# Scores by query in a transformer block: sixteen products of 32 by 32 in place of four of 32 by 128

## The chip, the cores and the metric

The kernel runs on one core of one Trainium2 chip. The metric is the device time of one execution in microseconds; shorter is better.

## The reference

A transformer block with adaptive layer norm (a condition gives shift, scale and gate for each of the two halves) on x of 8 x 1024 x 512, float32 throughout, 16 heads of 32 channels, causal attention, and a feed-forward part of 2048 channels:

```python
mod = silu(condition) @ Wada + bada
sh_a, sc_a, gt_a, sh_m, sc_m, gt_m = split(mod, 6, axis=1)
xn = layernorm(x, g1, be1)
xm = xn * (1 + sc_a) + sh_a
# attention, heads of 32 channels
scores = einsum('bhqd,bhkd->bhqk', q, k) * hd ** -0.5
attn = softmax(where(causal, scores, -inf))
out = einsum('bhqk,bhkd->bhqd', attn, v)
x = x + gt_a * (out @ Wproj + bproj)
xn = layernorm(x, g2, be2)
xm = xn * (1 + sc_m) + sh_m
h = gelu(xm @ W1 + b1)
x = x + gt_m * (h @ W2 + b2)
```

## The kernel before

The 8 sequences of 1024 tokens are cut into 16 blocks of 512 tokens (`n`; `h` says whether it is the first or the second block of its sequence). A block's queries and keys lie transposed in `qTs[n]` and `kTs[n]`: 128 partitions by 4 groups `g` by 512 tokens. A group is four heads, `HPG = 4`, of `hd = 32` channels, so head `j` of a group lies on the partitions 32j to 32j+31. In `qTs[n][r, gg, ...]` the slice `r` picks the head, `gg` the group, and the last index the tokens; `P` is 128, `TB` 512, and `SQ` (set for another purpose) 32.

Each softmax is made in two rounds. The first, scores by query, only finds the maximum of each row: `score_units` lists the work, `scores_at_once` (the edited function) makes scores with queries on the partitions and keys along the free dimension in `sc`, a tile of 128 x 4 x 512 that fills four PSUM banks, one for each head; VectorE adds the causal mask on the diagonal (L1745) and takes the maximum over the keys (L1748). The maxima are turned into rows (L1786). The second round, `weights_T`, makes the scores again with keys on the partitions (L1812 puts minus the maximum in, L1824 adds the scores) in `st`, ScalarE takes the exponential (L1837), GpSimd masks the diagonal and sums (L1842, L1950), and `weigh` multiplies by the values (L1865). `sc` and `st` share one buffer (the tag "st" has one).

One call of `scores_at_once` handles 512 columns of `sc` for a tile of 128 queries: one part of 512 columns, or on the diagonal 512, 384 + 128, or 256 + 256 columns (two groups). For each part it issues four products, one a head, whose stationary operand is 32 channels by 128 queries and whose moving operand is 32 channels by `w` keys. They occupy four separate row groups of TensorE's array. All linear layers (`matmul`, L233) instead use four products of 128 channels by 32 columns, in four column groups of the array; so do L1786, L1865 and L1886 (the sums of the weights). L1812 and L1824 use rows, like the scores.

The order of the work is written out by the kernel's own planner at build time: it keeps estimated times for each engine (`note_pe`, `note`), mixes the linear layers as a background stream with attention (`step_aside`, `work`, `pace`), and puts each step into the one queue of its engine. A stretch of scores therefore stands between stretches of linear layers.

Of the kernel before, what the change touches and what calls it, by code (L numbers as in the profile page):

```python
# [22 lines left out]
def kernel(  # L23
# [33 lines left out]
    nc = tc.nc  # L57
    B, T, D = x.shape
    HD = W1.shape[1]
    P = 128  # L60
    hd = D // H
# [6 lines left out]
    HPG = P // hd  # L68
# [62 lines left out]
    def note(engine, ns, reads=(), writes=(), port=False):  # L131
        start = max(now[engine], due(reads, writes))
        if port:
            start = max([start] + [b for a, b, *_ in pool_spans if a <= start < b])
            give_way(start, start + ns - FREE)
        elif engine == "POOL":
            start = max([start] + [b for a, b in port_spans if a <= start < b])
        end = start + ns
        now[engine] = end
        if port:  # L140
            port_spans.append((start, end - FREE))
            del port_spans[:-16]
        elif engine == "POOL":
            pool_spans.append((start, end, reads, writes))
            del pool_spans[:-16]
        for k in reads:
            left[k] = max(left.get(k, 0.0), end + SYNC)
        for k in writes:
            written[k] = end + SYNC
        return end  # L150

    def note_pe(ns, form, reads=(), writes=()):
        now["PE"] = max(now["PE"], due(reads, writes))
        if shape[0] != form:
            shape[0] = form
            now["PE"] += SWITCH
        note("PE", ns, reads)
        spent[0] += ns
        for k in writes:
            written[k] = now["PE"] + PIPE  # L160
# [80 lines left out]
    SQ = 32  # L241
# [43 lines left out]
    for w in range(1, NB):  # L285
        n = w - 1
# [26 lines left out]
    n = NB - 1  # L313
# [577 lines left out]
    qTs, kTs, vs = {}, {}, {}  # L891
# [699 lines left out]
    def step_aside(reads, writes):  # L1591


        while threads():
            if linear_wait() == NEVER:
                hurry()
            own, other = wait_of((reads, writes)), linear_wait()
            if done_linear[0] < stream["due"]:
                if other > own + 100:
                    break  # L1600
            elif own <= max(other, 50):
                break
            work()
        while BANK in writes and bank_at() == NEVER:
            work()
        run_jobs()
        run_pool_jobs()
        run_transfers()
        run_preparation()
# [52 lines left out]
    def keys_of(n, kh):  # L1662
        return kTs[n - blocks[n][1] + kh]

    def diagonals(parts, sc):

        if parts[-1][4] == parts[0][4]:
            first, span = parts[0][3] - P, len(parts) * P
            return span, sc[:, :, first : first + span]
        return 2 * P, sc.rearrange("p j (a c) -> p j a c", c=2 * P)[:, :, :, P:]  # L1670

    def scores(n, g, parts):

        h = blocks[n][1]
        for gg in {part[4]: None for part in parts}:
            if (n, gg) not in maxima:
                maxima[n, gg] = small.tile([P, 2, NTT, HPG], F32, tag="mx", name=f"mx_{n}_{gg}")
        reads = [("qT", n), ("kT", n - h + parts[0][1])]
        if (
            linear_wait() > 3000  # L1680
            and not any(live)
            and wait_of((reads, ["st"])) > wait_of((reads, [BANK])) + 1000
        ):
            scores_by_heads(n, g, parts, reads)
        else:
            scores_at_once(n, g, parts, reads)
        if units[unit_at[0] + 1 :] == [] or units[unit_at[0] + 1][:2] != (n, g):
            split_maxima(n, g, h)
# [35 lines left out]
    def scores_at_once(n, g, parts, reads):  # L1724
        h = blocks[n][1]
        step_aside(reads, ["st"])
        sc = ps_st.tile([P, HPG, TB], F32, tag="st", name=f"sc_{n}_{g}_{parts[0][0]}_{parts[0][1]}")
        for qt, kh, c0, w, gg in parts:
            for j in range(HPG):
                r = slice(j * hd, (j + 1) * hd)  # L1730
                nc.tensor.matmul(  # L1731
                    sc[:, j, c0 : c0 + w],
                    qTs[n][r, gg, ts(qt, P)],
                    keys_of(n, kh)[r, gg, :w],
                    start=True,
                    stop=True,
                    skip_group_check=True,
                )
            note_pe(2 * COLUMN * w, "rows", reads, ["st"])
        if parts[0][1] == h:  # L1740
            span, place = diagonals(parts, sc)
            shape_of = mask[:, :span].unsqueeze(1)
            if len(place.shape) == 4:
                shape_of = shape_of.rearrange("p o (a c) -> p o a c", c=P)
            nc.vector.tensor_tensor(place, place, shape_of.to_broadcast(place.shape), ALU.add)  # L1745
            note("DVE", 165 + 4.16 * span, ["st"])
        for qt, kh, c0, w, gg in parts:
            nc.vector.tensor_reduce(  # L1748
                maxima[n, gg][:, kh, qt, :], sc[:, :, c0 : c0 + w], axis=AX.X, op=ALU.max
            )  # L1750
            note("DVE", 170 + 4.14 * w, ["st"], [("mx", n, gg)])
# [383 lines left out]
```

## Time and profile before

| what | value |
|---|---|
| time, median of 3 runs | 3463.61 us (3462.65 to 3463.67) |
| the profiled execution | 3465.39 us, span of its trace 3463.7 us |
| granted TensorE clock | 0.999 |
| TensorE (PE) busy | 3424.3 us, 99% of the span |
| its weight loads (PEld) busy | 1776.1 us |
| VectorE (DVE), ScalarE (ACT), GpSimd (POOL) busy | 2069.1, 1288.6, 1940.4 us |
| passes of the edited line on TensorE | 329.2 us busy, 3072 records |

An instruction group is written as line, engine, operation, output and inputs by the program's tile names, output and input size (partitions x elements), number of instructions, then busy time in us, mean duration in ns, and the idle time ahead of it with what ended it. For TensorE a form such as `32*128` is the rows and columns of the array that an instruction uses, followed by the moving operand. PE are the passes of the moving operand, PEld the loads of the stationary one. In the timeline the first number is the start and the second the duration, from the first start to the last end of the merged instructions; passes overlap one another, since their ends include the way through the array.

### The profile page before, as it was taken

How to read it: one execution, taken by the hardware profiler on the slowest of the kernel's cores; microseconds unless marked ns; L12 is line 12 of the kernel's file. 1: busy time of each engine (PE TensorE's matmuls, PEld its weight loads, DVE VectorE, ACT ScalarE, POOL GpSimd, SP SyncE). 2: the span in 40 equal slices, each digit the busy share in tenths (PEclk: the TensorE clock that was granted, in tenths of full speed). 3: DMA queues.
4: the chain of work that ended last, by engine and by line, in shares of the span. 5: the costliest groups of instructions: out<-in, count | busy, mean ns of one | idle time of the engine just before them, and what ended most of it. 6: DMA issues, size and time to landing. Idle time of an engine off the chain costs nothing.

```text
span 3463.7 us, 122539 instructions
## 1 busy us (share of the span) xinstructions
PE 3424.3 (99%) x55442; PEld 1776.1 (51%) x55442; DVE 2069.1 (60%) x2295; ACT 1288.6 (37%) x1422; POOL 1940.4 (56%) x2090
## 2 busy tenths in 40 slices
PE   8999999999999999999999999999999999999999
PEld 5544554455544554455554455454554545544555
DVE  6765666646566465664657546575566745556364
ACT  2345234343243433434333352433524334242421
POOL 3666757756267572774626755277553774446530
PEclk9999999999999999999999999999999999999999
DMA  6843444345644455444544445444464454633444
GB/s 220 273 135 87 121 113 130 105 123 148 175 135 129 128 150 161 133 141 128 163 145 136 136 134 169 138 133 139 132 182 130 125 147 124 190 110 87 120 144 137
DMA packets 379613, 489.93 MB, mean 141 GB/s; under 512 B 28388, under 2 KB 235548, under 8 KB 379092
## 3 DMA queue, kind: packets, MB, share of 16 engines
q1 hardware_dynamic: 378896, 481.80, 47.1%
q8 instruction: 437, 7.16, 0.9%
q14 instruction: 84, 0.69, 0.1%
q10 hardware_dynamic: 196, 0.28, 0.0%
HBM read 428.44 MB, written 53.53 MB: 139 GB/s over the span
## 4 chain that ended last, share of the span: by engine, by line
PE 90%; DVE 4%; ACT 2%; DMA 2%; issue 1%; POOL 1%; SPq 0%; DVEq 0%; ACTq 0%; POOLq 0%
PE bank L233 62%; PE sc L1731 8%; PE po L1865 7%; PE st L1824 7%; PE st L1812 3%; DVE mx L1748 2%; PE bank L1886 2%; ACT pT L1837 1%; DMA w<-kept_up_S 1%; DVE sc L1745 1%; DMA xm_m<-turned_m 1%; PE bank L1786 1%; DVE hT L1321 0%; ACT hT L1252 0%; PE bank L847 0%
## 5 line engine op out<-in xcount | busy, mean ns | idle before, releaser
L1950 POOL TENSOR_TENSOR pT<-pT,pT 128x256 f32<-128x256 f32 (+3 forms) x1254 | 1221.5, 1009 | 148.5 <-ACT pT L1837 119.4
L1837 ACT ACTIVATE pT<-st 128x2048 f32<-128x2048 f32 x288 | 541.1, 1879 | 1006.9 <-PE st L1824 905.9
L233 PE MATMUL bank<-w,hT 128*32 128x256 f32 x14336 | 813.9, 380 | 0.0
L1748 DVE TENSOR_REDUCE mx<-sc 128x4 f32<-128x2048 f32 (+3 forms) x384 | 665.7, 1754 | 201.1 <-PE sc L1731 194.9
L233 PEld LDWEIGHTS bank<-w,hT 128*32 128x32 f32 x14336 | 454.4, 110 | 357.9 <-issue 75.7
L233 PE MATMUL bank<-xm_m,w 128*32 128x256 f32 x8192 | 499.5, 380 | 1.2 <-issue 0.7
L1842 POOL TENSOR_SCALAR_AFFINE_SELECT pT<-pT 128x512 f32<-128x512 f32 x256 | 180.5, 723 | 368.2 <-ACT pT L1837 366.4
L233 PE MATMUL bank<-t_m,w 128*32 128x256 f32 x6144 | 383.9, 381 | 1.0 <-DVE mx L1748 0.5
L233 PEld LDWEIGHTS bank<-xm_m,w 128*32 128x32 f32 x8192 | 256.4, 110 | 226.0 <-issue 60.9
L1731 PE MATMUL sc<-kT,qT 32*128 32x512 f32 (+3 forms) x3072 | 329.2, 520 | 3.5 <-DVE mx L1748 3.0
L1745 DVE TENSOR_TENSOR sc<-sc,mask 128x1024 f32<-128x1024 f32 (+1 forms) x160 | 162.8, 1017 | 250.7 <-PE sc L1731 179.4
L1865 PE MATMUL po<-pT,v 128*32 128x512 f32 (+3 forms) x3072 | 304.8, 491 | 0.5 <-POOL pT L1842 0.5
L1824 PE MATMUL st<-qT,kT 32*128 32x512 f32 (+3 forms) x3072 | 300.1, 486 | 0.0
L233 PEld LDWEIGHTS bank<-t_m,w 128*32 128x32 f32 x6144 | 190.0, 110 | 179.4 <-issue 53.1
L233 PE MATMUL bank<-xm_a,w 128*32 128x256 f32 x3968 | 241.0, 381 | 2.0 <-ACT xm_a L862 1.1
L190 POOL TENSOR_TENSOR qT<-top,rec 128x512 f32<-128x512 f32 x60 | 78.3, 1304 | 282.7 <-ACT rec L1904 279.0
L222 DVE TENSOR_TENSOR hT<-bank,u_u 128x512 f32<-128x512 f32 x192 | 130.2, 687 | 153.6 <-PE bank L233 151.0
L1731 PEld LDWEIGHTS sc<-kT,qT 32*128 32x128 f32 x3072 | 129.5, 183 | 162.1 <-issue 56.8
L233 PE MATMUL bank<-w,qT 128*32 128x256 f32 (+1 forms) x2944 | 192.4, 399 | 0.7 <-DVE p_proj L214 0.7
L233 PE MATMUL bank<-t_a,w 128*32 128x256 f32 x2944 | 179.4, 380 | 0.4 <-DVE qT L222 0.4
L233 PEld LDWEIGHTS bank<-xm_a,w 128*32 128x32 f32 x3968 | 127.7, 110 | 99.1 <-issue 17.9
L1252 ACT ACTIVATE hT<-hT,cols 128x512 f32<-128x512 f32 x256 | 164.1, 711 | 23.1 <-DVE hT L222 22.4
(238 smaller groups left out, 3408.4 us busy)
## 6 DMA issues: line engine op xcount, KB each, us to landing
w<-in_L_cond_W_dram SPq DMA_DIRECT2D x384, 256.0 KB
w<-kept_up_S SPq DMA_DIRECT2D x256, 256.0 KB
w<-kept_down_S SPq DMA_DIRECT2D x256, 256.0 KB
w<-kept_qkv_S SPq DMA_DIRECT2D x180, 256.0 KB
w<-in_L_cond_Wqkv_dram SPq DMA_DIRECT2D x147, 256.0 KB
hat<-in_x_dram SPq DMA_DIRECT2D x64, 256.0 KB
xr<-in_x_dram SPq DMA_DIRECT2D x64, 256.0 KB
out_dram<-xr SPq DMA_DIRECT2D x64, 256.0 KB
```

The source lines that it names most:

```text
L222: nc.vector.tensor_tensor(out, src, other, op)
L233: nc.tensor.matmul(ps[r], columns, rhs, start=start, stop=stop, skip_group_check=True)
L1252: nc.scalar.activation(hT[:, i, :], hT[:, i, :], AF.Gelu, bias=cols[:, O_B1 + f : O_B1 + f + 1])
L1731: nc.tensor.matmul(sc[:, j, c0 : c0 + w], qTs[n][r, gg, ts(qt, P)], keys_of(n, kh)[r, gg, :w], start=True, stop=True, skip_group_check=True,)
L1745: nc.vector.tensor_tensor(place, place, shape_of.to_broadcast(place.shape), ALU.add)
L1748: nc.vector.tensor_reduce(maxima[n, gg][:, kh, qt, :], sc[:, :, c0 : c0 + w], axis=AX.X, op=ALU.max)
L1812: nc.tensor.matmul(st[:, j, c0 : c0 + w], minus_ones[r, :], row[r, TB - w :], start=(c0 == 0), stop=False, skip_group_check=True,)
L1824: nc.tensor.matmul(st[:, j, c0 : c0 + w], kT[r, gg, ts(k % NTT, P)], qT[r, gg, TB - w :], start=False, stop=True, skip_group_check=True,)
L1837: nc.scalar.activation(pT[:, :, :used], st[:, :, :used], AF.Exp, scale=scale)
L1842: nc.gpsimd.affine_select(diagonal, diagonal, pattern=[[0, HPG], [1, P]], compare_op=ALU.is_ge, fill=0.0, base=0, channel_multiplier=-1,)
L1865: nc.tensor.matmul(po[r, TB - w :], v[:, k % NTT, g * P + j * hd : g * P + (j + 1) * hd], pT[:, j, c0 : c0 + w], start=(k == 0), stop=last ...
L1950: nc.gpsimd.tensor_tensor(into, into, pT[:, j, c0 : c0 + w], ALU.add)
```

## The change

Each of the four products of a part (32 channels by 128 queries) is split into four along the queries: sixteen products of 32 channels by 32 queries, each writing 32 partitions of one bank of `sc`. The outer loop goes over the four sets of 32 queries, the inner one over the four heads as before. What the planner is told (`note_pe`) is the same.

```diff
         for qt, kh, c0, w, gg in parts:
-            for j in range(HPG):
-                r = slice(j * hd, (j + 1) * hd)
-                nc.tensor.matmul(
-                    sc[:, j, c0 : c0 + w],
-                    qTs[n][r, gg, ts(qt, P)],
-                    keys_of(n, kh)[r, gg, :w],
-                    start=True,
-                    stop=True,
-                    skip_group_check=True,
-                )
+            for a in range(P // SQ):
+                for j in range(HPG):
+                    r = slice(j * hd, (j + 1) * hd)
+                    nc.tensor.matmul(
+                        sc[ts(a, SQ), j, c0 : c0 + w],
+                        qTs[n][r, gg, ts(qt * (P // SQ) + a, SQ)],
+                        keys_of(n, kh)[r, gg, :w],
+                        start=True,
+                        stop=True,
+                        skip_group_check=True,
+                    )
             note_pe(2 * COLUMN * w, "rows", reads, ["st"])
```

## The prediction

> **What bounds the kernel now.** I read the page first: the busy shares, the chain that ended last, and the costliest groups.
>
> ```profile
> span 3463.7 us, 122539 instructions
> PE 3424.3 (99%) x55442; PEld 1776.1 (51%) x55442; DVE 2069.1 (60%) x2295; ACT 1288.6 (37%) x1422; POOL 1940.4 (56%) x2090
> PE 90%; DVE 4%; ACT 2%; DMA 2%; issue 1%; POOL 1%; SPq 0%; DVEq 0%; ACTq 0%; POOLq 0%
> PE bank L233 62%; PE sc L1731 8%; PE po L1865 7%; PE st L1824 7%; PE st L1812 3%; DVE mx L1748 2%; PE bank L1886 2%; ACT pT L1837 1%; DMA w<-kept_up_S 1%; DVE sc L1745 1%; DMA xm_m<-turned_m 1%; PE bank L1786 1%; DVE hT L1321 0%; ACT hT L1252 0%; PE bank L847 0%
> L1837 ACT ACTIVATE pT<-st 128x2048 f32<-128x2048 f32 x288 | 541.1, 1879 | 1006.9 <-PE st L1824 905.9
> L1748 DVE TENSOR_REDUCE mx<-sc 128x4 f32<-128x2048 f32 (+3 forms) x384 | 665.7, 1754 | 201.1 <-PE sc L1731 194.9
> ```
>
> TensorE is busy 99% of the span and is 90% of the chain, so what the edited line L1731 takes on TensorE is paid almost one to one; it is 8% of the chain, some 280 us. The engines that consume the scores sit idle waiting for TensorE (the L1748 row: 194.9 of 201.1 us), so they set nothing here. How many stretches of scores there are I take from the instructions grouped with shapes kept apart:
>
> ```profile
> L1731 PE MATMUL sc<-kT,qT 32*128 32x512 f32 x1536 | 219.0, 640 | 2.7 <-DVE mx L1748 2.3
> L1731 PE MATMUL sc<-kT,qT 32*128 32x384 f32 x512 | 59.4, 533 | 0.0
> L1731 PE MATMUL sc<-kT,qT 32*128 32x256 f32 x512 | 36.7, 400 | 0.7 <-DVE mx L1748 0.7
> L1731 PE MATMUL sc<-kT,qT 32*128 32x128 f32 x512 | 25.6, 269 | 0.0
> L1731 PEld LDWEIGHTS sc<-kT,qT 32*128 32x128 f32 x3072 | 129.5, 183 | 162.1 <-issue 56.8 <-ACT pT L1837 45.0 <-DVE mx L1748 20.7
> ```
>
> Each program product is two records here, a first and a second pass over the moving operand (float32), each with its own weight load; a part of four products is 8 records. That makes 192 stretches of 512 columns alone, 64 of 384 + 128 and 32 of 256 + 256 (64 parts): 288 stretches of 512 columns each, one per call of scores_at_once, as many as the 288 exponentials of the transposed scores.
>
> **What one stretch costs.** The timeline of TensorE around one of the 192, then narrower windows on it, on its loads, and on a long stretch of L233.
>
> ```profile
> 1000.65 1.48 PE L233 MATMUL bank<-w,t 128*32 128x256 f32 x24
> 1002.06 1.14 PE L1731 MATMUL sc<-kT,qT 32*128 32x512 f32 x8
> 1003.13 0.64 PE L233 MATMUL bank<-w,t 128*32 128x256 f32 x8
> 1003.58 0.39 PE L233 MATMUL bank<-w,qT 128*32 128x256 f32 x3
> ...
> 1002.06 0.18 PEld L1731 LDWEIGHTS sc<-kT,qT 32*128 32x128 f32 x1 [0.41 <-ACT pT L1837]
> 1002.06 0.20 PEld L1731 LDWEIGHTS sc<-kT,qT 32*128 32x128 f32 x4 [0.41 <-ACT pT L1837]
> 1002.59 0.61 PE L1731 MATMUL sc<-kT,qT 32*128 32x512 f32 x4
> ...
> 1007.50 2.77 PE L233 MATMUL bank<-w,qT 128*32 128x256 f32 x48
> 1010.09 0.61 PE L1886 MATMUL bank<-pT,ones 128*32 128x512 f32 x4
> ```
>
> The 48 passes of L233 run from 1007.50 to 1010.09: six sets of eight (four side by side, twice) in 2.59 us, so 0.216 us for a pass of 256 columns and 0.43 for one of 512. The stretch of scores lasts from 1002.06 to 1003.13, 1.07 us: its first passes take 0.53 (1002.06 to 1002.59) and its second passes 0.54 until the next form may start. Over 2 x 0.43 that is 0.10 us of load in front (128 columns of queries, before anything streams) and 0.11 of emptying the array at the change of form, in which the last product's lag is contained. That lag: one load lasts 0.18, the four together 0.20, so three steps are 0.02 us, some 6.7 ns per product (5 to 8.3 by the rounding). The load of a form of 32 columns shows at 1003.13: its two passes of 256 columns last until 1003.58, 0.45 against 0.43 without a change of form, so 0.02 us.
>
> **The change, part by part.**
>
> Streaming. Four products of 32 by 128 fill the array; sixteen of 32 by 32 fill it too. All four row groups side by side are shown by L1731 itself, all four column groups by L233, and both at full rate. If all sixteen run side by side a pass stays 0.43 us: no change.
>
> The exposed load. It shrinks from 128 columns to 32: by the L233 entry it is 0.02 us in place of 0.10, minus 0.08 us per stretch, 23 us over 288.
>
> The stagger. Sixteen products start one behind the other where four did: fifteen steps in place of three, 12 x 6.7 ns = plus 0.08 us per stretch (0.06 to 0.10), 23 us over 288. It lies on the path, because the last product must finish before the form can change, and every stretch of scores has another form on both sides (L233 in the timeline). The step covers four instructions (load, pass, load, pass); I take it for products 5 to 16 as for 1 to 4, since nothing wider is in the trace, and keep both bounds.
>
> Within the 96 stretches of two parts the second part's loads and starts lie under the first part's passes (256 columns take 0.216 us, sixteen steps 0.11), so nothing is added.
>
> Instructions. L1731's 3072 passes and 3072 loads become 12288 of each, 18432 more instructions.
>
> ```profile
> q8 instruction: 437, 7.16, 0.9%
> L233 PEld LDWEIGHTS bank<-w,hT 128*32 128x32 f32 x14336 | 454.4, 110 | 357.9 <-issue 75.7
> 224.81 0.41 PE L1786 MATMUL bank<-ident_b,mcols 128*32 128x128 bf16 x16
> 225.03 0.61 PE L1865 MATMUL po<-pT,v 128*32 128x512 f32 x4
> ```
>
> 7.16 MB for 110884 loads and passes is 65 bytes each, so 1.2 MB more on a queue with a share of 0.9%: covered by the slack of the DMA engines. Later loads of 110 ns each lie beside passes as in L233. What is not covered is a slow feed of the 64 instructions at the head of a stretch. The fastest stretch that is dense throughout is L1786: 16 passes and 16 loads from 224.81 to 225.03, 6.9 ns per instruction, but there the passes themselves may be what sets it; the first four products of a stretch of scores take 1.7 ns per instruction (6.7 / 4). I take 1.7, which the nearer row shows, and keep 6.9 for a rival.
>
> The rest. The change moves no step, adds no DMA and no wait: the scores' tile, its readers, and the costs told to the planner are the same, so the written order on all engines stays. The maximum (L1748) and the mask (L1745) start after the last product as before.
>
> The sum: -0.08 + 0.08 = 0.00 us per stretch, between -0.02 and +0.02; over 288, between -6 and +6 us. The profiled execution took 3465.39 us with a span of 3463.7, 1.8 us over the median of 3463.61; I carry the difference to the median and forecast 3463 us. Something like 0.2%, 7 us, is what a measurement of this kernel tells from no change; that is 24 ns per stretch, or a step of 8.7 ns in place of 6.7.
>
> **The rivals.**
>
> Slower: the feed. TensorE's instructions arrive more slowly than 1.7 ns once the 16 at the head are used up. Product 16 has 60 instructions ahead of it; at 1.7 ns they take 0.10 us. From 2.1 ns on the loss is over 24 ns per stretch and the kernel is slower. At 3 ns product 16 starts at 0.18, +0.08 us, +23 us in all (3487); at the 6.9 ns of L1786 it starts at 0.41, +0.31, +90 us (3554). For it: four times the instructions come in the time that sixteen took, and no row shows 64 that fast. Against it: TensorE has 1.07 us of earlier work in which to run ahead. The Trainium skill (TensorE: Matmul & The Clock Gate, Part 1, on the 56 ns gap) has a floor that speaks against this change: starts of passes never come closer than about 25 ns. This trace does not agree, with four loads 0.02 us apart in all; by the page, 32 starts would last 0.8 us and a stretch about 1.3.
>
> Slower by much: waiting second passes hold up the products behind them. In the compiled program a product's second pass follows its first directly; that the four first passes nevertheless start within 0.02 us, and the second ones 0.53 later, shows that products on other tiles overtake up to three waiting passes. Whether they overtake fifteen, no row shows. If only four may wait, each set of four starts when the set before begins its second passes: five passes in place of two, +3 x 0.43 = 1.29 us, +370 us (3835). The Trainium skill (same page, Part 3, The mechanism) says that matmuls keep program order in start and end. The four here would then take five passes, 2.15 us, and they take 1.07, so the trace does not agree; for sixteen it would be seventeen passes.
>
> Faster: the step is shorter. The bfloat16 ones of L1812 start closer together:
>
> ```profile
> 1005.85 0.10 PEld L1812 LDWEIGHTS <-minus_ones 32*128 32x128 bf16 x4 [0.41 <-issue]
> L1812 PEld LDWEIGHTS <-minus_ones 32*128 32x128 bf16 x1536 | 31.5, 91 | 138.9 <-issue 89.3 <-DVE mx L1748 36.8 <-DVE mx L1762 2.5
> ```
>
> Four loads of 91 ns in 0.10 us are steps of 3 ns, for two instructions a product. If the step hangs on the product and not on its number of instructions, fifteen steps are 0.05 us, -0.05 net, -14 us (3449); if the lag costs nothing, because it lies under the emptying of 0.11, the whole load is won, -23 us (3440). The Trainium skill (same page, Part 3, measured speedup) gives about 4 ns per tile and a speedup of 10.6 for sixteen tiles; by it the gain would be about 12 us. No run here shows sixteen.
>
> That the change would not do what it says I see no room for: the slices are the same elements of queries, keys and scores.
>
> **How the numbers follow.** The forecast, balance within 6 us: 0.45. The feed: 0.25, most of it at the small end. Second passes that hold up: 0.10. The shorter step: 0.20. So faster 0.20, same 0.45, slower 0.35. The range from 3446 to 3492 holds the forecast, the faster case to beyond 3 ns a step, and the feed up to 3.3 ns per instruction; it leaves out the 0.10 of held-up passes, the costlier end of the feed (about 0.05) and the full gain of the load (about 0.05).
>
> **What would show it.** In the profile after, L1731 has 12288 passes and loads, of forms 32*32. Around one stretch the timeline should show the sixteen loads starting within 0.10 us, the second passes starting about 0.45 after the first, and the next form 1.07 after the beginning. Starts spread over more than 0.13 us show the feed; second passes of the first products before the first passes of the last show the hold-up, with a stretch of 2 us or more; a stretch under 1.04 shows the shorter step. The span's difference should be 288 times the stretch's difference; anything else, above all new waits on TensorE, would make this account wrong even where the time fits.

## The result

The changed kernel takes 3499.97 us (median of 4 runs, 3498.93 to 3502.4) against 3463.64 us before: slower by 36.3 us, a ratio of 1.0106 with a 95% interval of 1.0094 to 1.0119. The forecast was 3463, and the range ended at 3492.

The page of the changed kernel, the lines that answer to those shown of before (the edited line is now L1732):

```profile
span 3498.5 us, 140971 instructions
PE 3460.1 (99%) x64658; PEld 1774.9 (51%) x64658; DVE 2062.6 (59%) x2295; ACT 1288.8 (37%) x1422; POOL 1943.4 (56%) x2090
PE bank L233 64%; PE sc L1732 9%; PE po L1866 7%; PE st L1825 7%; PE st L1813 3%; PE bank L1887 2%; DVE mx L1749 2%; ACT pT L1838 1%; DMA w<-kept_up_S 1%; DMA xm_m<-turned_m 1%; PE bank L1787 0%; DVE sc L1746 0%; PE bank L847 0%; ACT hT L1252 0%; PE bank L582 0%
q8 instruction: 509, 8.34, 1.0%
L1732 PE MATMUL sc<-kT,qT 32*32 32x512 f32 (+3 forms) x12288 | 366.6, 492 | 3.1 <-DVE mx L1749 3.0
```

TensorE is still what bounds the kernel, with 36 us more of it busy; the other engines do what they did. The edited line alone is busy for 37 us more (366.6 after, 329.2 before). The passes by shape, shapes kept apart:

```profile
L1732 PE MATMUL sc<-kT,qT 32*32 32x512 f32 x6144 | 223.1, 599 | 2.8 <-DVE mx L1749 2.7
L1732 PE MATMUL sc<-kT,qT 32*32 32x384 f32 x2048 | 61.8, 493 | 0.0
L1732 PE MATMUL sc<-kT,qT 32*32 32x128 f32 x2048 | 52.8, 278 | 0.0
L1732 PE MATMUL sc<-kT,qT 32*32 32x256 f32 x2048 | 47.8, 385 | 0.3 <-DVE mx L1749 0.3
```

The calls of one part (512 columns) gained 4 us busy (219.0 before). The three shapes that occur only in calls of two parts gained 41 when their rows are added; 384 and 128 columns overlap in time, so this is more than the line gained as a whole. Among them the 128 columns, which come second, doubled (25.6 before). So the timeline is to be read in two places. First a call of one part: the whole of it, then cut off behind its first pass, behind the fourteenth, behind the sixteenth, and behind the seventeenth, which is the first of the second passes:

```profile
589.95 1.16 PE L1732 MATMUL sc<-kT,qT 32*32 32x512 f32 x32
591.04 0.85 PE L233 MATMUL bank<-w,qT 128*32 128x256 f32 x12
...
589.95 0.61 PE L1732 MATMUL sc<-kT,qT 32*32 32x512 f32 x1
589.95 0.70 PE L1732 MATMUL sc<-kT,qT 32*32 32x512 f32 x14
589.95 0.73 PE L1732 MATMUL sc<-kT,qT 32*32 32x512 f32 x16
589.95 1.04 PE L1732 MATMUL sc<-kT,qT 32*32 32x512 f32 x17
```

It lasts 1.09 us where it was 1.07 (1.087 and 1.071 in the trace's nanoseconds). All sixteen products run side by side. The first fourteen start within 0.09 us (0.70 less 0.61 for one pass), thirteen steps of 6.7 ns, and the last two need 0.03 for two more. The row with x17 is that of a view that closes at 590.41: the second passes begin 0.45 us into the call, 0.43 of streaming and 0.02 of load. Now a call of 384 + 128 columns, its passes, its loads, and its loads from the 35th on; below it one of before:

```profile
620.39 1.50 PE L1732 MATMUL sc<-kT,qT 32*32 32x384 f32 x64
621.81 0.42 PE L233 MATMUL bank<-w,hT 128*32 128x256 f32 x4
...
620.39 0.46 PEld L1732 LDWEIGHTS sc<-kT,qT 32*32 32x32 f32 x33 [0.41 <-ACT pT L1838]
621.06 0.55 PEld L1732 LDWEIGHTS sc<-kT,qT 32*32 32x32 f32 x31 [0.22 <-issue]
621.25 0.36 PEld L1732 LDWEIGHTS sc<-kT,qT 32*32 32x32 f32 x30
```

```profile
613.24 1.15 PE L1731 MATMUL sc<-kT,qT 32*128 32x384 f32 x16
614.32 0.42 PE L233 MATMUL bank<-w,hT 128*32 128x256 f32 x4
613.24 0.96 PEld L1731 LDWEIGHTS sc<-kT,qT 32*128 32x128 f32 x16 [0.41 <-ACT pT L1837]
```

This call takes 1.42 us where it took 1.08. Of its 64 loads, the 32 of the first part and one of the second come early, one more at 621.06, and the other thirty only from 621.25 on, 0.86 us into the call. Even the last tile had finished streaming the first part by then: twice 384 columns are 0.64 us, and the starts are spread over 0.12. And once they come they come slowly: thirty loads in 0.36 - 0.10 = 0.26 us, 17 ns for the four instructions of a product, 4.3 ns each, where the head of the call had 1.7. The view names no other engine that the loads waited for: it has "issue" (nothing that the profile shows) ahead of the one at 621.06, and nothing ahead of the thirty.

192 calls with 0.016 us more and 96 with 0.34 more are 3 + 33 = 36 us, which is the measured difference. Every one of the 96 shows the same wait.

### The profile page after: what moved, and what is told of

It reads as the page before. It is cut to its first block, busy times and chain, and to the rows that moved or that the text cites. A ratio compares the mean times of both kernels' runs of the same rounds, so it can differ in the third digit from the quotient of the medians.

```text
span 3498.5 us, 140971 instructions
## 1 busy us (share of the span) xinstructions
PE 3460.1 (99%) x64658; PEld 1774.9 (51%) x64658; DVE 2062.6 (59%) x2295; ACT 1288.8 (37%) x1422; POOL 1943.4 (56%) x2090
## 4 chain that ended last, share of the span: by engine, by line
PE 93%; DVE 3%; ACT 2%; DMA 1%; issue 1%; POOL 0%; SPq 0%; DVEq 0%; ACTq 0%; POOLq 0%
PE bank L233 64%; PE sc L1732 9%; PE po L1866 7%; PE st L1825 7%; PE st L1813 3%; PE bank L1887 2%; DVE mx L1749 2%; ACT pT L1838 1%; DMA w<-kept_up_S 1%; DMA xm_m<-turned_m 1%; PE bank L1787 0%; DVE sc L1746 0%; PE bank L847 0%; ACT hT L1252 0%; PE bank L582 0%
## 5 line engine op out<-in xcount | busy, mean ns | idle before, releaser
L1732 PE MATMUL sc<-kT,qT 32*32 32x512 f32 (+3 forms) x12288 | 366.6, 492 | 3.1 <-DVE mx L1749 3.0
L1732 PEld LDWEIGHTS sc<-kT,qT 32*32 32x32 f32 x12288 | 129.2, 103 | 176.6 <-issue 70.3
```

The costliest lines, as they stand in the source:

```text
L1732: nc.tensor.matmul(sc[ts(a, SQ), j, c0 : c0 + w], qTs[n][r, gg, ts(qt * (P // SQ) + a, SQ)], keys_of(n, kh)[r, gg, :w], start=True, stop=True,
```

## The experiments

Theory "window": TensorE takes in instructions in program order and holds about 64 of them, counted from the oldest one that is not finished. A part with sixteen products is 64 instructions (load, pass, load, pass for each). By the theory the second part of a call stays outside until products of the first are finished, and then comes in at the rate at which instructions are fed, 4.3 ns each. The call of 384 + 128 columns above shows where that comes from: the first product's second pass starts at 0.34 us (0.02 of load and 0.32 of streaming), and by the rows by shape a pass of 384 columns lasts 0.49 us with its way through the array, so this product is finished at 0.83; the held loads start at 0.86. (The ends of passes are modelled by the profiler, the starts are recorded.) Two rivals: "feed", a loss in proportion to the added instructions, and "same tiles", a second part that cannot follow the first closely on the same tiles of the array.

**e1_one_part and e2_two_part: the change in one kind of call alone.** The number of queries to a product is chosen by the kind of call:

```diff
-            for a in range(P // SQ):
+            SW = SQ if len(parts) == 1 else P      # e2: P if len(parts) == 1 else SQ
+            for a in range(P // SW):
...
-                        sc[ts(a, SQ), j, c0 : c0 + w],
-                        qTs[n][r, gg, ts(qt * (P // SQ) + a, SQ)],
+                        sc[ts(a, SW), j, c0 : c0 + w],
+                        qTs[n][r, gg, ts(qt * (P // SW) + a, SW)],
```

Expected of e1_one_part:

> Sixteen products only in the 192 calls of one part; four products, as before, in the 96 calls of two parts. Theory 'window': TensorE looks no further than about 64 instructions behind its oldest unfinished one, and a call of one part with sixteen products is just 64 instructions; it loses only the 16 ns that the trace after shows (1.087 us in place of 1.071), so +3 to +5 us, about 3467 us. Rival 'feed' (the loss goes with the number of added instructions, of which half are in these calls): half of the 36 us, about 3482 us. Rival 'same tiles' (a second part cannot follow the first closely on the same tiles of the array, whatever the number of instructions): as the window, 3467 us.

Expected of e2_two_part:

> Sixteen products only in the 96 calls of two parts, four in the others. Window: 128 instructions in a call, twice what TensorE looks over; the call takes 1.42 us in place of 1.08, so +33 us, about 3497 us. Feed: half of the 36 us, about 3482 us. Same tiles: 3497 us.

Measured: e1_one_part 3471.02 us, ratio 1.0019 (1.0010 to 1.0028); e2_two_part 3494.48 us, ratio 1.0088 (1.0074 to 1.0101). The two halves have the same number of added instructions and lose 7.4 and 30.8 us, so the loss does not go by instructions: feed alone is out. The losses add up, 38 for 36. The one-part kernel lost 7.4 us (3.5 to 9.7 by the interval) where 3 to 5 were expected; its trace shows 4.0 us more span than before (3467.7 us) and the same 1.087 us calls, so some 3 us of its median no view accounts for. "Same tiles" expects the same as the window of these two kernels; the next two tell them apart.

**e3_eight: eight products of 32 by 64 in every call.** Half the products, so that both parts of a call are 64 instructions:

```diff
-            for a in range(P // SQ):
+            SW = 2 * SQ
+            for a in range(P // SW):
```

> Eight products of 32 channels by 64 queries in every call. A part is 32 instructions, a call of two parts 64. Window: nothing waits beyond the window; the load in front is that of 64 columns (0.05 us, half of 0.10), the stagger seven steps of 6.7 ns (0.05) in place of three (0.02), so a call takes 1.04 us in place of 1.07 to 1.08, -0.03 x 288 = -8 us, about 3455 us: faster than before. Feed: a third of the added instructions of the sixteen (6144 of 18432), +12 us, less the 8: about 3468 us. Same tiles: the second part of the 96 calls waits as it does with sixteen, at least the 0.18 us by which its second product comes late there, +17 us, less the 8: about 3473 us.

Measured: 3456.41 us, ratio 0.9979 (0.9970 to 0.9988): 7.2 us faster than before, 43.6 faster than the change. Its timeline, a call of one part, one of 384 + 128 and that one's loads:

```profile
578.07 1.11 PE L1733 MATMUL sc<-kT,qT 32*64 32x512 f32 x16
579.11 0.42 PE L233 MATMUL bank<-w,qT 128*32 128x256 f32 x4
...
608.33 1.12 PE L1733 MATMUL sc<-kT,qT 32*64 32x384 f32 x32
609.38 0.42 PE L233 MATMUL bank<-w,hT 128*32 128x256 f32 x4
608.33 0.88 PEld L1733 LDWEIGHTS sc<-kT,qT 32*64 32x64 f32 x32 [0.41 <-ACT pT L1839]
```

1.04 and 1.05 us: the second part follows the first without a pause on the same tiles, so "same tiles" is out for tiles of 32 by 64. Both rivals had this kernel slower than before; only the window had it faster. The gain of 0.03 us per call fits the load of 64 columns in place of 128, less the stagger of eight products in place of four, as the expectation sums them.

**e4_sets_outside: the same instructions in another order.** In calls of two parts each set of 32 queries has both its parts before the next set begins:

```diff
         for qt, kh, c0, w, gg in parts:
-            for a in range(P // SQ):
+            note_pe(2 * COLUMN * w, "rows", reads, ["st"])
+        for a in range(P // SQ):
+            for qt, kh, c0, w, gg in parts:
                 for j in range(HPG):
...
-            note_pe(2 * COLUMN * w, "rows", reads, ["st"])
```

The planner is told the same for each part, now ahead of the products.

> Sixteen products, but in the calls of two parts the loop over the four sets of 32 queries stands outside the loop over the parts; the same instructions in another order. Window: the first 64 instructions now hold both parts of two sets, so the other two sets start only when products of the first sets are finished, at about 0.85 and 1.1 us; a call of two parts takes about 2.1 us in place of 1.42, +0.7 x 96 = +69 us over the changed kernel, about 3569 us. Feed: the same number of instructions, 3500 us. Same tiles: the sets that have not started wait for no tile, so at most as long as now, 3500 us or less.

Measured: 3566.7 us (one run). A call of 384 + 128 columns:

```profile
634.97 2.22 PE L1734 MATMUL sc<-kT,qT 32*32 32x384 f32 x64
637.12 0.42 PE L233 MATMUL bank<-w,hT 128*32 128x256 f32 x4
...
634.97 0.85 PEld L1734 LDWEIGHTS sc<-kT,qT 32*32 32x32 f32 x34 [0.41 <-ACT pT L1839]
635.83 1.10 PEld L1734 LDWEIGHTS sc<-kT,qT 32*32 32x32 f32 x30
...
635.12 0.10 PEld L1734 LDWEIGHTS sc<-kT,qT 32*32 32x32 f32 x1
635.50 0.10 PEld L1734 LDWEIGHTS sc<-kT,qT 32*32 32x32 f32 x1
```

It takes 2.15 us. Half of the array has nothing to do, the loads for it are next in the program, and yet thirty of them start only from 0.86 us on, as in the changed kernel, behind the 64 instructions of the first two sets. What holds them is their place in the program, not their tile.

The last two rows are the two loads of the third set's first product, the seventeenth, alone in narrow windows. Its first load is over at 0.26 us and its tile is idle, but its first pass, instruction 66, starts only at 0.53, with the second load right behind it. Instruction 2, 64 places before that pass, is the first pass of the call, which ends at about 0.50 (0.49 us by its row by shape); instruction 4, the second pass of the same product, ends at 0.83, and the loads from instruction 69 on start at 0.86. In all 64 calls of this shape both steps lie 0.03 us behind the end of that earlier pass. So places are given back one after the other in program order, and 64 is their number as these calls show it; 32 passes would be the same count, since here every pass has a load of its own.

**e5_halves16 and e6_halves4: calls of one part as two halves of 256 keys.** Is it the number of instructions, or the diagonal and the second group that are special to calls of two parts?

```diff
+            SW = SQ                                # e6: SW = P
+            pieces = [(0, w)] if len(parts) > 1 else [(0, w // 2), (w // 2, w // 2)]
+            for k0, kw in pieces:
-            for a in range(P // SQ):
+                for a in range(P // SW):
...
-                        sc[ts(a, SQ), j, c0 : c0 + w],
-                        qTs[n][r, gg, ts(qt * (P // SQ) + a, SQ)],
-                        keys_of(n, kh)[r, gg, :w],
+                            sc[ts(a, SW), j, c0 + k0 : c0 + k0 + kw],
+                            qTs[n][r, gg, ts(qt * (P // SW) + a, SW)],
+                            keys_of(n, kh)[r, gg, k0 : k0 + kw],
```

Expected of e5_halves16:

> The changed kernel with sixteen products in every call, and the 192 calls of one part issued as two halves of 256 keys each: 128 instructions where there were 64, the same work, one group of heads, one tile of queries. Window: these calls come to 1.42 us like those of 256 + 256 columns, in place of 1.087, +0.337 x 192 = +65 us over the changed kernel, about 3565 us, with the second half's loads after the first starting only about 0.64 us into the call. If what slows the calls of two parts is the diagonal's shape or the second group in them and not the number of instructions: no change, about 3500 us.

Expected of e6_halves4:

> The control: the same halves with four products of 32 by 128, so 32 instructions in a call. Window: nothing waits; the calls come to 1.076 us like those of 256 + 256 columns before, in place of 1.071, +1 us, about 3465 us. If halving itself costs (twice the passes, whatever their number in the window): a good part of the 65 us of its sister, 3480 us or more.

Measured: e5_halves16 3560.65 us, ratio 1.0280 (1.0261 to 1.0298), 61 us over the changed kernel; e6_halves4 3464.23 us beside 3464.18 before, ratio 1.000 (0.999 to 1.001). One call of each:

```profile
604.63 1.49 PE L1735 MATMUL sc<-kT,qT 32*32 32x256 f32 x64
606.05 0.42 PE L233 MATMUL bank<-w,qT 128*32 128x256 f32 x4
```

```profile
580.12 1.15 PE L1735 MATMUL sc<-kT,qT 32*128 32x256 f32 x16
581.19 0.42 PE L233 MATMUL bank<-w,qT 128*32 128x256 f32 x4
```

1.42 us for 128 instructions and 1.07 for 32, for the same products of one group and one tile of queries. Halving costs nothing while it fits.

Where the window ends can be read from calls of 256 + 256 columns in the changed kernel, in which every pass is 0.11 us shorter than one of 384 columns. If the second part waits for the first product to be finished, the held loads must come two passes, 0.21 us, sooner than at 0.86:

```profile
629.31 1.49 PE L1732 MATMUL sc<-kT,qT 32*32 32x256 f32 x64
630.74 0.42 PE L233 MATMUL bank<-w,hT 128*32 128x256 f32 x4
629.96 0.37 PEld L1732 LDWEIGHTS sc<-kT,qT 32*32 32x32 f32 x30
```

They come at 629.96, 0.65 us into the call: 0.21 sooner. The release goes with the end of the first product and not with a fixed delay; in all 96 calls of two parts the held loads start 0.03 us after it. No run varied the limit itself, and that 4.3 ns is the rate of the feed is inferred: nothing else in the views sets the pace of the held loads.

## Why the prediction was wrong

- **What bounds the kernel** held: TensorE pays almost one to one, 36 us busy for 36 us of time.
- **Streaming** held: sixteen products side by side keep the pass at 0.43 us. The held-up second passes (370 us and more) did not occur; fifteen waiting passes are overtaken as three are. The Trainium skill's rule of program order for starts and ends (TensorE: Matmul & The Clock Gate, Part 3, The mechanism) is not what this trace shows, with sixteen first passes under way within 0.12 us and the second ones from 0.45 on.
- **Load and stagger** held nearly: thirteen of the fifteen steps are the 6.7 ns of the prediction, and the load in front shrank to 0.02 us as forecast. The last two products came some 15 ns apart, fed late, which makes the 0.016 us that the call lost. e3_eight shows the two terms at other sizes, and they balance to -0.03 us as these sums have it.
- **The step that failed** is the sentence on the 96 calls of two parts: that the second part's loads and starts lie under the first part's passes, so that nothing is added. It compared only times, 0.216 us of pass with 0.11 of starts, and took for granted that the second part's instructions are already there. They are not: the first part alone fills what TensorE holds. This cost 0.34 us in each, 33 of the 36 us. Of the signs that the prediction named, those for one stretch nearly came true, since they describe a call of one part; its last sign, the span's difference as 288 times the stretch's, did not (288 x 0.016 is 5 us, the spans differ by 35), and it is the one that points to the other calls.
- **The feed rival** had the right family and the wrong place and price. It set the danger at the head of a call, where the 64 instructions lay ready but for those of the last two products, and spread it over 288 calls; it sits behind the 64th and falls on 96. Instructions do come at 4.3 ns once the store is used up, within the 1.7 to 6.9 that were kept as bounds. At 4.3 ns the rival's own sum gives +0.16 us in each of 288 calls, 45 us; that this lies near the 36 measured is chance. The Trainium skill (TensorE: Matmul & The Clock Gate, the table at its top) gives TensorE's queue a depth of 64; the thirty loads held in e4_sets_outside and the changed kernel agree with that number. The floor of 25 ns between starts that the prediction cites from the Trainium skill (TensorE: Matmul & The Clock Gate, Part 1) does not show here: sixteen starts lie within 0.12 us.

## What to carry to other kernels

When products are cut finer for TensorE's array, count instructions and not only columns: by these runs, what has to run at the same time must lie within about 64 consecutive instructions, and a float32 product counts four. Up to there finer products cost a stagger of 7 ns each and save load time in front; beyond it the later ones wait for the oldest to finish. Here eight products of 32 by 64 (3456.41 us) beat both four and sixteen: they save more load than they add stagger, and both parts of a call just fit.

## What the runs showed of the hardware

Sixteen float32 products of 32 by 32 run fully side by side on this chip: 32 passes of 512 columns in 1.09 us with load and drain. Instructions that wait behind the 64th come only as the oldest ones finish (0.03 us after, in 96 of 96 calls), and then at about 4.3 ns each, against 1.7 ns for those that lie ready. And an idle half of the array does not draw work from behind that window (e4_sets_outside, 2.15 us for the work of 1.08).
